# Changes between parts of the TensorE array, weighed by kind and put off by up to 100 places, in a macaron transformer kernel

## The chip, the core and the metric

The kernel runs on one core of one Trainium2 chip. A core has engines that run their own instruction streams and wait for one another by semaphores: TensorE (PE in the profile; its weight loads are the row PEld) multiplies matrices into PSUM, a buffer of eight banks; VectorE (DVE), ScalarE (ACT) and GpSimd (POOL) work on vectors; SyncE (SP) issues DMAs. The metric is the time of one execution on the device in microseconds (us), as the median of several runs. All data is 32-bit floating point.

## The reference

The input `x` is eight sequences of 512 tokens with 256 channels. Three residual parts follow one another, each on a layer-normalized copy:

```python
x = x + 0.5 * _L0_ffn_ref(_layernorm(x), ...)
x = x + _L0_attn_ref(_layernorm(x), L0_attn_weight)
x = x + 0.5 * _L0_ffn_ref(_layernorm(x), ...)
```

`_L0_ffn_ref` is two layers of a local-attention block. In each, half of the channels are shifted by a token, a product with `wqkv` gives queries, keys and values for 8 heads of 64 channels, queries and keys are normalized, scaled and rotated, and each window of 128 tokens attends to itself and to the window before it. A product with `wo` is added; then comes a gated feed-forward part with 682 hidden channels (`w1`, GELU, `w2`).

`_L0_attn_ref` is global attention with 16 heads of 16 channels, in which queries and keys are the same: `scores = y @ y.T / 4`, a softmax over 512 tokens, a product with all 256 channels of the layer-normalized `x`, and for each head a 256x256 slice of `weight`, summed over the heads.

## The kernel before

**Streams.** The program is recorded first and ordered afterwards. Three generators record it: two block streams (`stream`, one for the even and one for the odd sequences), each with `attention` and `glu` for two layers, and the stream of the global heads (`global_heads`). They are stepped in turn, so that the records of all three are interleaved. The first block stream is six steps ahead of the second.

**Products and the parts of the array that they use.** TensorE is an array of 128x128. Most products use it whole: the product with `wqkv` (`front` in `attention`), with `wo` (`project`), with `w1` and `w2` (`glu`), the heads' products with `weight` (`project` in `global_heads`) and their weighted sums (`attend`), and the transposes. Three kinds use a part, and several of them run side by side in the array:

- scores of the local attention (`scores` in `attention`): 64 rows, two heads at a time; one recorded operation has four products and fills two PSUM banks. The last 42 hidden channels with their bias row (`glu`, 43 rows) belong to the same kind. This text calls it halves.
- probabilities times values (`values`): 64 columns, two heads at a time. Called columns.
- scores of the global heads (`scores` in `global_heads`): 16 rows, four products at a time into four banks. Called fours.

One product of the source is two instructions in the profile, and a transpose is one. What is recorded under `plan.together()` is one operation and is issued without a break.

**What follows the small products.** After local scores, VectorE adds the mask and takes row maxima, ScalarE computes the exponentials, and GpSimd (or VectorE) scales them. Except for the first and the last sequences of each stream, the probabilities are turned by VectorE and by DMAs through DRAM (`turned_far`); there, TensorE transposes them. The values product follows, then the product with `wo`. The probabilities have two buffers a stream, so the scores of the next tokens need those of the tokens before to have been used. After global scores, ScalarE computes four exponentials, which `attend` of that head reads; the exponentials have eight buffers, two heads' worth.

**The planner.** `Plan.order` is a list scheduler with a cost model (`Plan.cost`). Each operation has a rank, its place in the order of recording. The planner keeps a clock for each engine, and at each step it takes the engine whose earliest candidate can start first, then among the candidates that can start within 40 ns of that one it takes the lowest rank. To the rank, `STICK` places are added where the candidate needs a change of mode: on ScalarE another activation table, on TensorE another part of the array. `MODE` is the time that the planner's clock adds for such a change. The mode of a product is set in `cost`: before, it is "rows" for up to 64 rows, "columns" for up to 64 columns and "whole" otherwise, so that halves and fours are one mode. A candidate that opens more than four buffers and whose inputs are ready, which the scores of a global head are, holds back all candidates of a higher rank that open a PSUM bank (`hold`).

The order that comes out is fixed for all five queues, SyncE's DMA issues among them, and each engine runs its own in that order.

Of the kernel before, what the change touches and what calls it, by code (L numbers as in the profile page):

```python
# [167 lines left out]
def elements(a):  # L168
    n = 1
    for d in a.shape[1:]:  # L170
        n *= d
    return n


class Plan:
    ENGINES = ("tensor", "vector", "scalar", "gpsimd", "sync")
    SIGNAL = 110.0
    TABLE = 1283.0
    STICK = {"tensor": 4, "scalar": 12, "vector": 0, "gpsimd": 0, "sync": 0}
    MODE = 130.0  # L180

    def __init__(self):
        self.ops, self.stream, self.group, self.shift = [], None, None, 0.0
# [46 lines left out]
    def cost(self, op):  # L230

        if op.engine == "tensor":

            lanes, op.mode = {}, "whole"
            for name, args, kw in op.calls:
                lane, t = 0, 109.0
                if name == "matmul":
                    a = kw["lhsT"]
                    lane, t = (a.region()[0], args[0].region()[0]), 2 * max(0.842 * elements(kw["rhs"]), 109.0)
                    op.mode = "rows" if a.shape[0] <= 64 else "columns" if a.shape[1] <= 64 else "whole"  # L240
                lanes[lane] = lanes.get(lane, 0.0) + t
            busy = max(lanes.values())
            return busy, busy + 170
        name, args, kw = op.calls[0]
        n = max(elements(a) for a in (*args, *kw.values()) if hasattr(a, "shape"))
        if name == "dma_start":
            return 580.0, 2300.0
        if op.engine == "scalar":
            if name == "activation":
                op.mode = {AF.Exp: "exp", AF.Gelu: "gelu"}.get(args[2])  # L250
                busy = 70 + 0.82 * n + (105 if "bias" in kw else 0)
                return (busy + 93, busy + 310) if "accum_out" in kw else (busy, busy + 110)
            return 70 + 0.81 * n, 175 + 0.81 * n
        if op.engine == "vector":
            if name == "tensor_tensor_reduce":
                return 90.0 + n, 250.0 + n
            if name == "bn_stats":
                return 70.0 + n, 150.0 + n
            return 90 + 1.035 * n, 170 + 1.035 * n
        if name == "memset":  # L260
            return 80 + 0.85 * n, 100 + 0.85 * n
        if ALU.pow in args:
            return 350.0 + 157 * n, 400.0 + 157 * n
        return 210 + 1.98 * n, 250 + 1.98 * n

    def order(self):

        for op in self.ops:
            op.busy, op.done = self.cost(op)
            op.waits = len(op.after)  # L270
            for o in op.after:
                o.before.append(op)

            for t in op.tiles:
                if t.users[0] is op:
                    source = [] if t.ring.space == PSUM else [u for u in op.tiles if u.ring.space == PSUM and u.users[0] is not op]
                    (source[0].users[0] if source else op).opens.append(t)
        for op in self.ops:
            op.opens.sort(key=lambda t: t.turn)
            for t in op.opens:  # L280
                for o in t.users:
                    if o is not op:
                        op.admits.append(o)
                        o.waits += 1
        free, mode = dict.fromkeys(self.ENGINES, 0.0), dict.fromkeys(self.ENGINES)
        pipe = 0.0
        candidates = {e: [op for op in self.ops if op.engine == e and not op.waits] for e in self.ENGINES}
        order = []

        def slots(op):  # L290

            need, turns, at = {}, {}, 0.0
            for t in op.opens:
                k, i = need.get(t.ring, 0), turns.get((t.ring, t.stream), 0)
                need[t.ring], turns[t.ring, t.stream] = k + 1, i + 1
                if t.ring.space != PSUM:

                    k += t.ring.missing(t.stream, t.turn) - i
                if len(t.ring.free) <= k:
                    return None  # L300
                at = max(at, t.ring.free[k][0])
            return at

        while len(order) < len(self.ops):
            best = None
            for e in self.ENGINES:
                when = []
                hold = min((op.rank for op in candidates[e] if len(op.opens) > 4 and op.ready <= free[e]), default=None)
                for op in candidates[e]:
                    if op.opens:  # L310
                        at = slots(op)
                        if at is None:
                            continue
                        if hold is not None and op.rank > hold and op.opens[0].ring.space == PSUM:
                            continue
                        at = max(at, op.ready, free[e])
                    else:
                        at = max(op.ready, free[e])
                    when.append((at, op))
                if when:  # L320
                    t = min(at for at, _ in when)
                    if best is None or t < best[0]:
                        best = t, e, when
            assert best is not None, "the plan is stuck"
            t, e, when = best
            change = {"tensor": self.MODE, "scalar": self.TABLE}.get(e, 0.0)
            switch = lambda op: change if op.mode is not None and op.mode != mode[e] else 0.0
            at, op = min(
                ((at, op) for at, op in when if at <= t + 40), key=lambda c: (c[1].rank + (self.STICK[e] if switch(c[1]) else 0), c[0])
            )  # L330
            candidates[e].remove(op)
            op.start = at + switch(op)
            mode[e] = op.mode or mode[e]
            free[e] = op.start + op.busy
            op.end = op.start + op.done
            if op.calls[0][0] == "dma_start":
                a = op.calls[0][2]["out"]
                pipe = max(pipe, op.start + 2000.0) + elements(a) * a.shape[0] * 4 / 170
                op.end = pipe + 300
            for x in op.opens:  # L340
                _, x.slot = x.ring.free.pop(0)
                x.ring.open(x.stream, x.turn)
            for x in op.tiles:
                x.left -= 1
                x.end = max(x.end, op.end)
                if not x.left:
                    x.ring.free.append((x.end + self.SIGNAL, x.slot))
                    x.ring.free.sort()
            for o in op.before:
                if o.engine != e:  # L350
                    o.ready = max(o.ready, op.end + self.SIGNAL)
                elif e != "tensor":
                    o.ready = max(o.ready, op.end)
            for o in op.before + op.admits:
                o.waits -= 1
                if not o.waits:
                    candidates[o.engine].append(o)
            order.append(op)
        return order
# [661 lines left out]
```

## Time and profile before

| | |
|---|---|
| median of 3 runs | 4,106.5 us (4,104.8 to 4,114.1) |
| profiled execution | 4,109.5 us |
| its span, first to last instruction | 4,107.8 us |
| granted TensorE clock, mean | 0.996 of full speed |
| TensorE instructions | 19,968 matmuls, 4,028.8 us busy |
| VectorE, ScalarE, GpSimd busy | 2,479.5, 1,866.7, 1,291.2 us |
| mean share of the DMA engines, main queue | 29.0% |

How to read it: an engine's busy time is the union of its instructions' records. For TensorE the ends of the records are modelled, so how close its instructions follow one another is read from their starts. In the groups and in the order of time, `128*64 128x128` says that 128 rows and 64 columns of the array are used, and that the result is 128 partitions by 128 elements; `psum_bank<-work_p,work_v` names the output and the inputs by the tiles of the program. Since all instructions are issued from one helper, all have the line L365, and the tiles tell them apart: `work_kT,work_qT` are local scores, `work_p,work_v` and `work_pT,work_v` are values, `work_hT` are global scores, `work_xw,work_e` is `attend`, `work_wa,work_gz` is the heads' product with `weight`, `wpool_w` is the feed-forward part and `wpool_wqkv` and `wpool_wo` are the products around local attention. What stands in brackets is idle time ahead of an instruction and what ended it.

### The profile page before, as it was taken

The page shows a single profiled execution, that of the slowest core. Times are in us where ns is not written, and L with a number is a line of the kernel's source. Part 1 is how long each engine was busy: PE and PEld are TensorE (multiplying, and loading weights), DVE is VectorE, ACT ScalarE, POOL GpSimd, SP SyncE. Part 2 cuts the span into 40 slices and gives each one's busy share as a digit, 9 for nine tenths or more (in the row PEclk, how much of TensorE's full clock was granted, in tenths as well). Part 3 has the DMA queues.
Part 4 walks back from the last instruction along what each step waited for, and adds up shares of the span by engine and source line. Part 5 has one row for each costly group of instructions (what it writes and reads, how often), then busy time and mean ns, then how long its engine had stood idle before and what let it go on. Part 6 is the DMA issues. An engine that isn't in the chain of part 4 may idle for free.

```text
span 4107.8 us, 59405 instructions
## 1 busy us (share of the span) xinstructions
PE 4028.8 (98%) x19968; PEld 2739.1 (67%) x19968; DVE 2479.5 (60%) x6760; ACT 1866.7 (45%) x4606; POOL 1291.2 (31%) x1147
## 2 busy tenths in 40 slices
PE   7999999999999999999999999999999999999998
PEld 4565676666666667666676766667676666686655
DVE  7575655756557565574756656567547565535574
ACT  5665444444444344443444544444324344323664
POOL 5242423424234232341523324234214232103140
PEclk9999999999999999999999999999999999999999
DMA  3001433423334243342433423334224243210000
GB/s 112 1 22 45 126 113 104 137 88 121 117 105 147 63 132 110 100 158 70 148 115 98 157 74 118 113 108 151 81 60 148 77 136 100 67 33 11 1 22 11
DMA packets 378704, 379.93 MB, mean 92 GB/s; under 512 B 48320, under 2 KB 323360, under 8 KB 378400
## 3 DMA queue, kind: packets, MB, share of 16 engines
q1 hardware_dynamic: 377536, 374.81, 29.0%
q8 instruction: 159, 2.61, 0.3%
q10 hardware_dynamic: 864, 1.33, 0.1%
q14 instruction: 145, 1.19, 0.1%
HBM read 216.61 MB, written 142.61 MB: 87 GB/s over the span
## 4 chain that ended last, share of the span: by engine, by line
PE 81%; DVE 9%; ACT 6%; issue 2%; POOL 1%; DMA 0%; SPq 0%; DVEq 0%; ACTq 0%; POOLq 0%
PE psum_bank L365 81%; ACT work_p L365 3%; DVE work_qn L365 3%; DVE work_p L365 2%; DVE small_ss L365 1%; ACT L365 1%; DVE work_both L365 0%; POOL small_rn L365 0%; DVE xpool_x L365 0%; ACT work_qn L365 0%; DVE small_nmax L365 0%; DVE small_bnst L365 0%; POOL work_t L365 0%; DVE zpool_z L365 0%; SPq L365 0%
## 5 line engine op out<-in xcount | busy, mean ns | idle before, releaser
L365 PE MATMUL psum_bank<-work_xw,work_e 128*128 128x256 f32 x4096 | 977.5, 384 | 6.8 <-DVE work_xw L365 4.3
L365 PEld LDWEIGHTS psum_bank<-work_xw,work_e 128*128 128x128 f32 x4096 | 759.4, 190 | 203.0 <-issue 67.4
L365 PE MATMUL psum_bank<-wpool_wqkv,zpool_z 128*128 128x512 f32 x1536 | 705.1, 599 | 3.3 <-DVE xpool_x L365 1.5
L365 ACT ACTIVATE work_p<-work_p,small_nmax,small_rn 128x256 f32<-128x256 f32 (+1 forms) x1024 | 574.2, 563 | 284.4 <-DVE small_nmax L365 146.9
L365 POOL TENSOR_TENSOR work_t<-work_qn,const_tab 128x256 f32<-128x256 f32 x512 | 391.1, 785 | 700.0 <-ACT work_qn L365 698.5
L365 POOL TENSOR_TENSOR work_p<-work_p,small_ri 128x1024 f32<-128x1024 f32 (+1 forms) x192 | 334.5, 1744 | 834.3 <-DVE small_ri L365 370.3
L365 PE MATMUL psum_bank<-zpool_z,wpool_w 128*128 128x512 f32 x1280 | 566.0, 596 | 1.4 <-DVE zpool_z L365 1.4
L365 ACT ACTIVATE work_e<-psum_bank 128x512 f32<-128x512 f32 x512 | 297.9, 595 | 485.3 <-PE psum_bank L365 480.8
L365 POOL TENSOR_TENSOR small_rn<-small_ss,const_nhalf 128x8 f32<-128x8 f32 x256 | 483.4, 1890 | 89.2 <-DVE small_ss L365 80.7
L365 PE MATMUL psum_bank<-work_wa,work_gz 128*128 128x256 f32 x2048 | 491.3, 383 | 10.1 <-DVE work_gz L365 5.6
L365 PEld LDWEIGHTS psum_bank<-wpool_wqkv,zpool_z 128*128 128x128 f32 x1536 | 284.4, 191 | 299.9 <-issue 273.6
L365 DVE SCALAR_TENSOR_TENSOR xpool_x<-psum_bank,gsmall_rinv,xpool_x 128x256 f32<-128x256 f32 x512 | 242.0, 474 | 343.1 <-PE psum_bank L365 340.4
L365 PEld LDWEIGHTS psum_bank<-work_wa,work_gz 128*128 128x128 f32 x2048 | 381.8, 190 | 82.5 <-issue 17.7
L365 PEld LDWEIGHTS psum_bank<-zpool_z,wpool_w 128*128 128x128 f32 x1280 | 240.5, 190 | 292.6 <-issue 263.6
L365 DVE CUSTOM_DVE_ANT_0 work_p<-psum_bank,const_mask 128x256 f32<-128x256 f32 (+1 forms) x1024 | 339.2, 383 | 46.6 <-PE psum_bank L365 45.2
L365 ACT COPY work_qn<-psum_bank 128x512 f32<-128x512 f32 x256 | 146.7, 582 | 363.0 <-PE psum_bank L365 328.4
L365 DVE COPY work_xw<-psum_bank 128x512 f32<-128x512 f32 x256 | 174.3, 682 | 156.2 <-PE psum_bank L365 155.9
L365 ACT ACT_TABLE_LOAD x158 | 202.7, 1283 | 143.2 <-DVE small_nmax L365 60.1
L365 DVE TENSOR_REDUCE small_ss<-work_sq 128x8 f32<-128x512 f32 x256 | 173.0, 676 | 145.3 <-ACT work_sq L365 145.0
L365 POOL TENSOR_TENSOR small_rstd<-small_ve,const_nhalf 128x4 f32<-128x4 f32 x48 | 49.8, 1037 | 648.1 <-DVE small_ve L365 616.1
L365 PE MATMUL psum_bank<-wpool_wo,work_o 128*128 128x256 f32 x1024 | 247.3, 385 | 2.5 <-ACT work_o L365 2.4
L365 PE MATMUL psum_bank<-wpool_w,work_p 128*128 128x256 f32 x1024 | 247.7, 385 | 0.0
(81 smaller groups left out, 5009.2 us busy)
## 6 DMA issues: line engine op xcount, KB each, us to landing
dram_turned<-work_p SPq DMA_DIRECT2D x144, 512.0 KB
work_p<-dram_turned SPq DMA_DIRECT2D x576, 128.0 KB
dram_turned<-work_both SPq DMA_DIRECT2D x96, 512.0 KB
work_both<-dram_turned SPq DMA_DIRECT2D x384, 128.0 KB
work_wa<-in_weight_dram SPq DMA_DIRECT2D x128, 256.0 KB
wpool_w<-in_w_dram SPq DMA_DIRECT2D x48, 640.0 KB
work_hT<-work_gz SPq DMA_DIRECT2D x512, 32.0 KB
dram_turned<-work_p SPq DMA_DIRECT2D x48, 256.0 KB
```

Source lines behind the costliest of these rows:

```text
L365: getattr(getattr(nc, op.engine), name)(*map(real, args), **{k: real(a) for k, a in kw.items()})
```

## The change

Three things change in the planner, and nothing in what is recorded. `STICK` for TensorE goes from 4 to 100 places. The mode of a product has four kinds in place of three: up to 32 rows are "fours", up to 64 "halves". And the time of a change is taken by the kind that is left: 150 ns, or 290 ns when fours are left, in place of 130 ns for all. The program has the same instructions in another order.

```diff
-    STICK = {"tensor": 4, "scalar": 12, "vector": 0, "gpsimd": 0, "sync": 0}
-    MODE = 130.0
+
+    STICK = {"tensor": 100, "scalar": 12, "vector": 0, "gpsimd": 0, "sync": 0}
+    MODE = {"whole": 150.0, "columns": 150.0, "halves": 150.0, "fours": 290.0}
...
-                    op.mode = "rows" if a.shape[0] <= 64 else "columns" if a.shape[1] <= 64 else "whole"
+                    k, m = a.shape
+                    op.mode = "fours" if k <= 32 else "halves" if k <= 64 else "columns" if m <= 64 else "whole"
...
-            change = {"tensor": self.MODE, "scalar": self.TABLE}.get(e, 0.0)
+            change = self.MODE.get(mode[e], 0.0) if e == "tensor" else self.TABLE if e == "scalar" else 0.0
```

The line behind the last one, which is as it was, makes a change of any candidate whose mode is not the engine's present one, and adds the stick to its rank.

## The prediction

> **What bounds the kernel now.** I read the page first: the busy shares, the chain that ended last, the groups by form; then the TensorE instructions in order of time, then the list of TensorE's waits.
>
> ```profile
> span 4107.8 us, 59405 instructions
> PE 4028.8 (98%) x19968; PEld 2739.1 (67%) x19968; DVE 2479.5 (60%) x6760; ACT 1866.7 (45%) x4606; POOL 1291.2 (31%) x1147
> ...
> PE 81%; DVE 9%; ACT 6%; issue 2%; POOL 1%; DMA 0%; SPq 0%; DVEq 0%; ACTq 0%; POOLq 0%
> ```
>
> TensorE is busy for 98% of the span, no other engine for more than 60%, and 81% of the chain runs over it. But its ends are modelled, so 98% does not say what fills the time. Start times do. These are the TensorE instructions of one stretch in order (start, length, what, count, idle before):
>
> ```profile
> 1511.04 1.89 PE L365 MATMUL psum_bank<-work_xw,work_e 128*128 128x256 f32 x8
> 1512.77 1.89 PE L365 MATMUL psum_bank<-work_wa,work_gz 128*128 128x256 f32 x8
> 1514.49 1.89 PE L365 MATMUL psum_bank<-work_xw,work_e 128*128 128x256 f32 x8
> 1516.31 1.09 PE L365 MATMUL psum_bank<-work_p,work_v 128*64 128x128 f32 x16
> 1517.34 1.14 PE L365 MATMUL psum_bank<-work_hT 16*128 16x512 f32 x8
> 1519.92 1.99 PE L365 MATMUL psum_bank<-work_wa,work_gz 128*128 128x256 f32 x8 [1.44 <-DVE xpool_x L365]
> 1521.85 1.09 PE L365 MATMUL psum_bank<-work_p,work_v 128*64 128x128 f32 x16
> 1522.87 3.72 PE L365 MATMUL psum_bank<-work_xw,work_e 128*128 128x256 f32 x16
> 1526.52 0.66 PE L365 MATMUL psum_bank<-work_p,work_v 128*64 128x128 f32 x8
> ```
>
> Eight instructions of 128x256 on the whole array take 1.73 us from start to start when whole products stand on both sides (1511.04 to 1512.77), so 0.216 us each. The eight ahead of a product on half the columns (128\*64) take 1.82 (1514.49 to 1516.31): 0.09 more. The sixteen between two half-column products take 3.65 (1522.87 to 1526.52) where 16 x 0.216 is 3.45: 0.10 for the second start after coming back, and 0.09 for leaving. That is the price of a change between parts of the array.
>
> I took the starts of all 19,968 matmul records in order and put each distance against that form's own. The distances are 0.216 (256 columns, whole), 0.429 (512), 0.109 (a transpose); products that share the array start 0.007 apart, and a pair then takes 0.216 or 0.112 (64 rows) or 0.109 (half columns), and four of 16 rows 0.429. By kind, the extra of a visit is:
> - columns: 0.093 + 0.051 on entering, 0.100 + 0.104 on returning, 0.35 us
> - halves (64 or 43 rows): 0.093 + 0.104 and 0.096 + 0.104, 0.40 us
> - fours (16 rows): 0.093 + 0.104 and 0.109 + 0.104, 0.41 us
>
> There are 1,055 changes: 489 excursions from the whole array, in which 208 runs of halves, 231 of columns and 127 of fours stand. Their extras add up to **196 us**, 0.185 each. The rest of the span: the work at its own distances 3,783 (8,704 x 0.216 + 2,816 x 0.429 + 1,536 x 0.109 + the small products' 527), ahead of the first matmul and after the last start 19, and 110 left over, which is waiting, 77 of it in 90 single waits. The sum is 4,107.8. Of those waits only 33 us lie between 300 and 3,700 us; the rest is the beginning and the end. TensorE is thus bound by its own issue, and changes are 4.8% of the span.
>
> ```profile
> PE psum_bank L365 <- DVE work_qn L365: 19.3, 19, 3.1
> PE psum_bank L365 <- DVE ypool_y L365: 16.2, 3, 12.8
> PE psum_bank L365 <- DVE xpool_x L365: 7.6, 7, 1.5
> ```
>
> (us in total, times, longest.) No wait is large, and the longest is the first.
>
> **The change, part by part.** It adds and removes no instruction. It changes the order that the planner writes out, on all five queues, since one engine's pick decides when the next one's inputs are ready.
>
> *The stick of 100 places.* A place is one recorded operation. There are about 16,100: DVE 6,760 less 1,024 accumulator reads, ACT 4,606 less 1,536 reads and 158 table loads, POOL 1,143, some 2,260 DMA issues on SP, and 4,060 on TensorE. So 100 places are 0.62% of the span, **25.5 us**; the 4 places of before are 1 us. Before, TensorE left the whole array for nearly any older small product, and 168 excursions are a single run of columns, 154 of halves, 94 of fours. Now it stays whole until a ready small product is 100 places older than every ready whole one, or until no whole one is ready. Meanwhile small products pile up and go together, and as all of them are changes by then, the next kind follows the first: k kinds cost k + 1 changes, not 2k.
>
> How many remain? The floor of one change is as it was; only the count moves. I cut the span into windows and let each be one excursion through the kinds that occur in it: windows of 25.5 us leave 497 changes, of 16 us 635, of 13 us 704. The full 25.5 us is reached by no average product: many are old when they become ready (a far block's probabilities come back by DMA), whole products run out at times, and the hold of the planner lets the heads' scores (fours, 128, one every 32 us) pass later-ranked bank users. I take the 16 us windows, **640 changes**: 415 fewer, 415 x 0.185 = **-77 us**. Ends: 497 (-103) and 900 (-29).
>
> *What the moved products drag along.* Scores and values come up to 25 us later, and so do their evictions (DVE row maxima, ACT exponentials, POOL scaling), the DMAs that SP issues for the turned probabilities (one of 512 KB and four of 128 KB for most pairs) and the next scores, which need the probabilities' buffers back. SP's queue is in order, so a late turn also stands ahead of later weight and head loads. All of this is hidden as long as TensorE has other whole products ready: its waits of 33 us in 3,400 show that it nearly always has. If that cover goes, a late value is next waited for by the projection and then by the feed-forward part of that block, at 1 to 3 us each, the longest of the first row above.
>
> *Bunching.* Here a rule of the Trainium skill speaks against the change. TensorEngine Tiling (Array Packing), under PSUM Bottleneck and Gotcha 1: PSUM Pressure, says that splitting the array speeds up TensorE but not the emptying of PSUM, and that row tiles fill different banks. The rows agree on sizes: a scores product fills two banks in 0.9 us and DVE empties them in 4 x 0.417 plus reads, 2.0 us; a head's scores fill four in 1.1 us and ACT needs 4 x (0.595 + 0.206) = 3.2 us:
>
> ```profile
> L365 ACT ACTIVATE work_e<-psum_bank 128x512 f32<-128x512 f32 x512 | 297.9, 595 | 485.3 <-PE psum_bank L365 480.8 <-issue 4.5
> ...
> L365 DVE CUSTOM_DVE_ANT_0 work_p<-psum_bank,const_mask 128x256 f32<-128x256 f32 x768 | 280.5, 417 | 34.8 <-PE psum_bank L365 33.5 <-DMA work_both<-dram_turned 0.3
> ```
>
> Two scores products and a head in a row take all eight banks. By the rule each of the 128 heads would then end in a wait like that at 1519.92 (1.44 us, columns and fours ahead of it): +184 us, and the whole would be 4,107.8 - 77 + 184 = 4,215. By the trace, the 50 excursions of two or three runs between 300 and 3,700 us already show what bunches do: they and the 3 us behind them hold 0.106 us of waits each, single ones 0.025. With some 200 excursions of mostly two or three runs, that is about 20 us in place of the 14 that lie there now; bunches get larger than today's, so I take **+20 us**, with 0 and +120 as ends. The measured rate weighs more than the rule, as DVE and ACT empty banks side by side and neither is over 60% busy.
>
> *The kinds and their prices* (rows split into halves and fours; 150 and 290 ns in place of 130). A change between halves and fours occurs 11 times now and costs 0.2 like any other, so treating it as one is right; the prices only move planned start times. They come nearer to the 0.185 measured. I cost this at 0, from -5 to +5.
>
> *ACT's rule* stays, so 158 table loads stay near that; at 1.28 us each they lie in ACT's idle 55%.
>
> Sum against the profiled execution: 4,107.8 - 77 + 20 = 4,050.8 of span, plus 1.7 around it (4,109.5 in all before). That execution is 3.0 above the median of the runs, 4,106.5; a difference of -57 makes **4,050**.
>
> **The rivals.**
> 1. *Fuller bunches without waits*: 497 changes and no new wait, -103: 4,003. For it: the backlog that the small number of waits shows. Against: the windows assume perfect batches.
> 2. *Bunches starve PSUM* (slower): -77 is 0.39 us for each of 200 excursions. If a wait of 1.5 us follows more than one in four, the gain is gone; at one in two, +150: 4,180. For it the rule and the line at 1519.92, against it 0.106 us as measured.
> 3. *Late streams*: the two block streams fall 25 us behind the heads, and the end, where only they are left and waits are dense already (12 us of the last 108 without a busy TensorE), grows by that; with the beginning +40, so 4,107 - 77 + 20 + 40, about 4,090. Against: when no whole product is ready, the rule does not hold a small one back.
> 4. *The order hardly changes*, because same-kind products are seldom ready: 950 changes, -19, so 4,087; with new waits of that size, no change. Against: whole products are ready nearly always, so most departures could have been put off.
>
> **How the numbers follow.** Forecast 0.54 (its own range 4,015 to 4,085), fuller bunches 0.15, starving 0.16, late streams 0.08, hardly a change 0.07. The range of 8 in 10 goes from 3,990, a little under rival 1 for windows wider than 25.5 us, to 4,135, where waits of 1.5 us follow a third of the excursions (+100). A measurement of this kernel tells about 0.2%, 8 us. Faster: 0.54 + 0.15 + 0.07 of late streams + 0.03 of rival 4, 0.79, less 0.04 for the forecast's own upper tail, 0.75. Same 0.06, the rest of rival 4 and a little. Slower 0.19: starving, and that tail.
>
> **What the changed profile would show.** Right: changes down to 550 to 750, each still at 0.18 to 0.21; runs of 32 and more columns instructions and of 24 and more halves in the order of time; instruction counts as before; TensorE's waits below 140 us in all. The starving rival: many lines with over 1 us of idle behind fours or halves, released by ACT work_e, DVE work_p or xpool_x. Late streams: the last 100 us longer with waits on work_qn and work_pT. What would make me wrong is a planner that meets the bunches with banks full, or a count that stays above 900.

## The result and the profile after

The changed kernel takes **4,056.0 us** (median of 4 runs, 4,055.9 to 4,056.2) against 4,105.9 us for the kernel before (here over 4 runs): a ratio of 0.9874 with a 95% interval of 0.9857 to 0.9891. The forecast was 4,050. The time is right; two terms of the sum behind it are not, and they cancel.

The head of the page of the changed kernel:

```profile
span 4054.2 us, 59391 instructions
PE 3986.8 (98%) x19968; PEld 2747.4 (68%) x19968; DVE 2461.8 (61%) x6760; ACT 1822.8 (45%) x4566; POOL 1277.5 (32%) x1147
```

The matmuls are the same 19,968. TensorE is still busy for 98% of the span, and its issue is still the bound: by the starts, work and changes fill 3,946 of the 4,054 us (table below). Its instructions in order of time, in about the same stretch as before (start, length, what, count; what was L365 is L367 now):

```profile
1513.32 1.14 PE L367 MATMUL psum_bank<-work_kT,work_qT 64*128 64x256 f32 x8
1514.38 1.09 PE L367 MATMUL psum_bank<-work_p,work_v 128*64 128x128 f32 x16
1515.41 1.99 PE L367 MATMUL psum_bank<-work_xw,work_e 128*128 128x256 f32 x8
1517.24 1.89 PE L367 MATMUL psum_bank<-work_wa,work_gz 128*128 128x256 f32 x8
1519.06 1.09 PE L367 MATMUL psum_bank<-work_p,work_v 128*64 128x128 f32 x16
1520.08 1.14 PE L367 MATMUL psum_bank<-work_hT 16*128 16x512 f32 x8
1521.15 1.99 PE L367 MATMUL psum_bank<-wpool_wo,work_o 128*128 128x256 f32 x8
```

Two things are seen. The price of a change is what it was: the eight products behind the columns take 1.83 us (1515.41 to 1517.24), 0.10 more than 1.73, and the eight ahead of the next columns 1.82. And small products of different kinds now stand behind one another (halves and columns, then columns and fours), so two kinds cost three changes. But the two products of columns, 4.7 us apart, were not brought together.

The list of TensorE's waits (us in total, times, longest):

```profile
PE psum_bank L367 <- DVE work_qn L367: 17.9, 35, 3.1
PE psum_bank L367 <- DVE ypool_y L367: 17.6, 6, 12.9
PE psum_bank L367 <- DVE work_p L367: 6.9, 3, 3.1
```

The first two rows are about as before, and the 7.6 us behind xpool_x are gone from the list.

I took the span apart as in the prediction, from the starts of all matmuls: 3,783 us of work at its own distances, changes, the ends, and what is left, which is waits and stretches at half clock. Where a wait covers a change, the change is counted here at its usual price (so 198 us for before, where the prediction had 196).

| kernel | changes | us in changes | ends | left over | of it, clock not granted | span |
|---|---|---|---|---|---|---|
| before | 1,055 | 197.9 | 18.6 | 108.4 | 16.5 | 4,107.8 |
| after | 885 | 162.9 | 19.6 | 88.8 | 11.4 | 4,054.2 |
| difference | -170 | -35.0 | +1.0 | -19.6 | -5.1 | -53.6 |

The clock column is one minus the mean granted clock, times the span; a little of it falls into waits or into the ends, so it is not wholly a part of what is left over. So 35 us of the gain came from fewer changes and 20 from less waiting and half clock. With one fixed price for each kind of change, taken from the prediction's list, the same traces give 34 and 21; in x4 below, the split would move by 7 us, in x8 by 6, in the others by less.

### The profile page after: what moved, and what is told of

It is laid out like the page before. It is cut to its first block, busy times and chain, and to the rows that moved or that the text cites. A ratio compares the mean times of both kernels' runs of the same rounds, so it can differ in the third digit from the quotient of the medians.

```text
span 4054.2 us, 59391 instructions
## 1 busy us (share of the span) xinstructions
PE 3986.8 (98%) x19968; PEld 2747.4 (68%) x19968; DVE 2461.8 (61%) x6760; ACT 1822.8 (45%) x4566; POOL 1277.5 (32%) x1147
## 4 chain that ended last, share of the span: by engine, by line
PE 45%; DVE 3%; ACT 2%; POOL 1%; issue 0%; DMA 0%; SPq 0%; DVEq 0%; ACTq 0%; POOLq 0%
PE psum_bank L367 45%; ACT work_p L367 1%; DVE work_p L367 1%; DVE work_qn L367 1%; POOL small_rn L367 0%; DVE ypool_y L367 0%; DVE small_ss L367 0%; DVE xpool_x L367 0%; POOL work_t L367 0%; DMA work_both<-dram_turned 0%; DVE small_bnst L367 0%; POOL small_rstd L367 0%; ACT work_pT L367 0%; ACT work_qn L367 0%; ACT work_sq L367 0%
## 5 line engine op out<-in xcount | busy, mean ns | idle before, releaser
L367 PE MATMUL psum_bank<-work_xw,work_e 128*128 128x256 f32 x4096 | 957.1, 383 | 3.9 <-DVE work_xw L367 1.9
L367 PEld LDWEIGHTS psum_bank<-work_xw,work_e 128*128 128x128 f32 x4096 | 761.0, 190 | 190.5 <-issue 52.1
L367 ACT ACTIVATE work_p<-work_p,small_nmax,small_rn 128x256 f32<-128x256 f32 (+1 forms) x1024 | 574.0, 562 | 295.3 <-DVE small_nmax L367 218.4
L367 PE MATMUL psum_bank<-wpool_wqkv,zpool_z 128*128 128x512 f32 x1536 | 703.9, 596 | 0.3 <-ACT zpool_z L367 0.3
L367 POOL TENSOR_TENSOR work_p<-work_p,small_ri 128x1024 f32<-128x1024 f32 (+1 forms) x192 | 327.3, 1707 | 1038.2 <-DVE small_ri L367 595.6
L367 POOL TENSOR_TENSOR work_t<-work_qn,const_tab 128x256 f32<-128x256 f32 x512 | 383.9, 770 | 755.4 <-ACT work_qn L367 748.9
L367 PE MATMUL psum_bank<-zpool_z,wpool_w 128*128 128x512 f32 x1280 | 559.6, 595 | 1.5 <-DVE zpool_z L367 1.4
L367 POOL TENSOR_TENSOR small_rn<-small_ss,const_nhalf 128x8 f32<-128x8 f32 x256 | 484.2, 1893 | 129.9 <-DVE small_ss L367 124.1
L367 PE MATMUL psum_bank<-work_wa,work_gz 128*128 128x256 f32 x2048 | 475.5, 380 | 2.1 <-DVE work_gz L367 1.3
L367 DVE SCALAR_TENSOR_TENSOR xpool_x<-psum_bank,gsmall_rinv,xpool_x 128x256 f32<-128x256 f32 x512 | 242.1, 475 | 386.3 <-PE psum_bank L367 383.6
L367 ACT ACTIVATE work_e<-psum_bank 128x512 f32<-128x512 f32 x512 | 298.5, 596 | 395.7 <-PE psum_bank L367 386.1
L367 PEld LDWEIGHTS psum_bank<-wpool_wqkv,zpool_z 128*128 128x128 f32 x1536 | 284.2, 191 | 274.8 <-issue 256.2
L367 PEld LDWEIGHTS psum_bank<-zpool_z,wpool_w 128*128 128x128 f32 x1280 | 242.5, 191 | 301.8 <-issue 274.9
L367 PEld LDWEIGHTS psum_bank<-work_wa,work_gz 128*128 128x128 f32 x2048 | 384.4, 190 | 67.9 <-issue 10.2
L367 DVE CUSTOM_DVE_ANT_0 work_p<-psum_bank,const_mask 128x256 f32<-128x256 f32 (+1 forms) x1024 | 339.2, 385 | 115.5 <-PE psum_bank L367 114.6
L367 ACT COPY work_qn<-psum_bank 128x512 f32<-128x512 f32 x256 | 148.6, 583 | 426.3 <-PE psum_bank L367 368.5
L367 DVE TENSOR_REDUCE small_ss<-work_sq 128x8 f32<-128x512 f32 x256 | 173.3, 677 | 176.5 <-ACT work_sq L367 176.2
L367 DVE SCALAR_TENSOR_TENSOR work_p<-psum_bank,const_vec,work_p 128x512 f32<-128x512 f32 x128 | 95.9, 750 | 263.4 <-PE psum_bank L367 162.4
L367 PE MATMUL psum_bank<-wpool_wo,work_o 128*128 128x256 f32 x1024 | 248.4, 386 | 0.9 <-ACT work_o L367 0.7
L367 DVE COPY work_xw<-psum_bank 128x512 f32<-128x512 f32 x256 | 173.9, 680 | 116.0 <-PE psum_bank L367 114.7
L367 PE MATMUL psum_bank<-wpool_w,work_p 128*128 128x256 f32 x1024 | 242.9, 380 | 0.4 <-ACT work_e L367 0.4
L367 PE MATMUL psum_bank<-work_kT,work_qT 64*128 64x256 f32 (+1 forms) x2048 | 236.1, 364 | 1.8 <-DVE work_xw L367 1.4
```

Of the source, the lines that this page charges most:

```text
L367: getattr(getattr(nc, op.engine), name)(*map(real, args), **{k: real(a) for k, a in kw.items()})
```

## The experiments

All are orders of the same work: they compute everything. "Changes" and "left over" are taken from each one's trace as above. Time is the median, and the ratio is to the kernel before on the same chip. Each trace is one execution, and the twenty executions of x12 alone lie between 4,110.3 and 4,117.1 us, so a few us of what is left over say nothing.

| run | stick | prices, ns | changes | us in changes | left over | clock not granted | us | ratio (95%) |
|---|---|---|---|---|---|---|---|---|
| x8 | -100 | 130 | 1,379 | 255.2 | 81.1 | 14.4 | 4,136.3 | 1.0069 (1.0053 to 1.0085) |
| x12 | 2 | 130 | 1,056 | 199.9 | 112.5 | 23.1 | 4,114.6 | 1.0016 (1.0009 to 1.0023) |
| x2 | 4 | by kind | 1,059 | 198.2 | 109.2 | 14.8 | 4,108.9 | 0.9998 (0.9989 to 1.0007) |
| x5 | 50 | 130 | 940 | 173.7 | 96.4 | 14.9 | 4,073.2 | 0.9911 (0.9894 to 0.9929) |
| x6 | 99 | 130 | 872 | 161.3 | 75.7 | 7.9 | 4,042.6 | 0.9838 (0.9823 to 0.9853) |
| x1 | 100 | 130 | 874 | 161.4 | 72.6 | 6.4 | 4,039.7 | 0.9828 (0.9809 to 0.9847) |
| x3 | 100 | 130, four kinds | 890 | 163.9 | 84.3 | 12.9 | 4,050.9 | 0.9855 (0.9836 to 0.9875) |
| x11 | 100 | as measured | 876 | 161.0 | 107.6 | 16.8 | 4,073.4 | 0.9914 (0.9899 to 0.9929) |
| x7 | 150 | 130 | 817 | 151.6 | 98.5 | 18.3 | 4,056.2 | 0.9871 (0.9855 to 0.9886) |
| x10 | 150 | as measured | 804 | 148.5 | 93.2 | 11.4 | 4,047.3 | 0.9853 (0.9836 to 0.9869) |
| x9 | 175 | as measured | 817 | 149.4 | 97.1 | 8.3 | 4,051.7 | 0.9862 (0.9848 to 0.9877) |
| x4 | no limit | by kind | 751 | 135.1 | 155.4 | 35.5 | 4,091.4 | 0.9957 (0.9941 to 0.9973) |

### The parts of the change alone

Theory A: the stick does all, through the number of changes. Theory B: the prices by kind bring the planned clock nearer to the chip's, and so the waits fell. The stick alone, x1:

```diff
-    STICK = {"tensor": 4, "scalar": 12, ...}
+    STICK = {"tensor": 100, "scalar": 12, ...}
     MODE = 130.0
```

> The kernel before with the stick of 100 places alone (rows stay one kind, 130 ns for every change). Its order has 874 changes, 11 fewer than the changed kernel's 885. Theory A, the stick does it all by the number of changes, and the drop of 20 us in waits comes with it or by chance: about 4,054 us, changes 160 us, waits near 90. Theory B, the prices by kind bring the planned clock nearer to the chip's and so take the waits down: changes 160 us as well, but waits stay near 110, about 4,073 us.

4,039.7 us, better than either theory said and better than the whole change. The head of its page and its list of waits:

```profile
span 4036.4 us, 59364 instructions
```

```profile
PE psum_bank L365 <- DVE ypool_y L365: 18.7, 7, 12.8
PE psum_bank L365 <- DVE work_qn L365: 13.6, 21, 3.1
PE psum_bank L365 <- ACT work_pT L365: 7.3, 11, 1.6
```

The changes cost what they do in the changed kernel (161 and 163 us); what is left over is 16 us less. The first line has one wait of 12.8 us at the beginning that all kernels have (12.8 in before, 12.9 after, 13.6 in x4), so what shrinks lies elsewhere.

Kinds and prices alone, x2:

```diff
-    STICK = {"tensor": 100, "scalar": 12, ...}
+    STICK = {"tensor": 4, "scalar": 12, ...}
```

> The changed kernel with the stick back at 4 places: four kinds and the prices of 150 and 290 ns alone. Its order has 1,059 changes, as many as before (1,055). Theory A: about 4,106 us, as before. Theory B: changes 196 us, waits near 90, about 4,087 us.

The same as before within 0.1%: as many changes, and as much left over. Theory B falls: with a stick of 4, the prices by kind took no wait away.

The changed kernel with one price, x3:

```diff
-    MODE = {"whole": 150.0, "columns": 150.0, "halves": 150.0, "fours": 290.0}
+    MODE = {"whole": 130.0, "columns": 130.0, "halves": 130.0, "fours": 130.0}
```

> The changed kernel with 130 ns for every change, the four kinds and the stick of 100 kept; 890 changes in its order. Theory A: 4,057 us. Theory B: waits back near 110, about 4,075 us.

4,050.9 us; waits do not go back up. Against B again. With x1 and x2 this puts the gain on the stick.

### No limit

x4 puts small products off until nothing else can start:

```diff
-    STICK = {"tensor": 100, "scalar": 12, ...}
+    STICK = {"tensor": 100000, "scalar": 12, ...}
```

> The changed kernel with a stick without limit: TensorE leaves a part of the array only when nothing of that kind can start. 751 changes in its order, 134 fewer. If the number of changes sets the time and waits stay at 90: 134 x 0.183 = 25 us less, about 4,031 us. If bunches and late streams cost waits once small products are put off without limit: waits of 130 us and more, 4,070 us or above.

4,091.4 us: 28 us saved in changes against the changed kernel, and 67 more left over. This run settles two points. First, by its rule TensorE leaves a part of the array only when nothing of that kind can start, and 751 changes are still made. So it is not the number of places that keeps bunches small. The planner of this kernel, followed step by step, says what does. At 233 of its 462 departures from a part, no other product of that kind is a candidate (not all that it needs has been placed in the order yet); at 63 there is one that can start only more than 40 ns later; at 166 there is one without a free buffer, and 117 of these are heads' scores, which lack mostly one of the eight buffers of the exponentials. Second, this run shows the rival of starved PSUM at work. The waits of this run, and its order of time around 1,285 us, where a new sequence of the heads' stream begins:

```profile
PE psum_bank L367 <- ACT work_e L367: 11.3, 6, 2.8
```

```profile
1283.12 1.99 PE L367 MATMUL psum_bank<-wpool_wo,work_o 128*128 128x256 f32 x8
1285.05 3.80 PE L367 MATMUL psum_bank<-work_hT 16*128 16x512 f32 x14
1291.63 2.07 PE L367 MATMUL psum_bank<-work_hT 16*128 16x512 f32 x2 [2.78 <-ACT work_e L367]
1293.63 0.47 PE L367 MATMUL psum_bank<-const_ident,ypool_y 128*128 128x128 f32 x1
```

Two heads' scores in a row fill eight banks, and the last product waits until ScalarE has emptied one. The kernel before has such a place too, at 1,311 us, with a shorter wait:

```profile
1311.05 2.05 PE L365 MATMUL psum_bank<-work_hT 16*128 16x512 f32 x10
1314.05 2.27 PE L365 MATMUL psum_bank<-work_hT 16*128 16x512 f32 x6 [0.95 <-ACT work_e L365]
```

The stages of x4, from 1,281 us on (busy us and count of each engine, then the granted clock, DMA share and GB/s), show what follows:

```profile
1281.00:1285.00 4.00, 3.88 (x24) 2.90 (x24) 2.83 (x8) 2.57 (x5) 3.89 (x5) 1.00 0.49 164
1285.00:1289.00 4.00, 3.85 (x15) 1.48 (x14) 4.00 (x19) 2.77 (x9) 1.17 (x2) 0.94 0.79 258
1289.00:1293.00 4.00, 1.37 (x2) 0.50 (x2) 4.00 (x6) 4.00 (x15) 2.52 (x2) 0.50 0.48 131
1293.00:1297.00 4.00, 4.00 (x10) 2.75 (x10) 2.75 (x5) 3.62 (x12) 3.46 (x2) 0.50 0.74 243
```

The clock is granted at half, and stays so for 10.2 us. Near 804, 2,125 and 3,442 us the order of time has nearly the same picture, with one transpose between the two heads, and each time a wait of 2.23 us. In all this run loses 35 us of clock, 24 more than the changed kernel. The waits on work_e (11 us) and the half clock behind these four places (17 us) are at most 28 of the 67 us; the rest is spread over other waits, and its cause is not shown.

### How far, and how much is chance

Theory C: the stick itself takes waits down as far as it puts small products off. Theory D: waits differ from order to order by chance. x5, x6, x7 and x8 are the kernel before with other sticks:

```diff
-    STICK = {"tensor": 4, "scalar": 12, ...}
+    STICK = {"tensor": 50, "scalar": 12, ...}
```

> The kernel before with a stick of 50; 940 changes in its order, 115 fewer than before, so 21 us less in changes. Theory C, the stick itself takes waits down as far as it puts small products off: about half of the 36 us that a stick of 100 took from the waits, so about 4,067 us. Theory D, waits differ from order to order by chance: anything between 4,050 (rest as with 100) and 4,085 (rest as before).

4,073.2 us, 12 of 36 us of waits gone. Theory C had 18 of them gone and is 6 us off; theory D allowed nearly anything, so this run does not decide between them.

```diff
+    STICK = {"tensor": 99, "scalar": 12, ...}
```

> The kernel before with a stick of 99 in place of 100: nearly the same rule, another order, 872 changes (874 with 100). Theory C: within 4 us of 4,040. Theory D, waits are a matter of chance: the rest outside work and changes may lie anywhere from 73 to 90 us, so 4,040 to 4,057; then the 16 us between the stick alone and the whole change say nothing of kinds and prices.

4,042.6 us, 3 us of left-over from x1: as theory C said, but inside the range of theory D as well.

```diff
+    STICK = {"tensor": 150, "scalar": 12, ...}
```

> The kernel before with a stick of 150; 817 changes, 57 fewer than with 100, so 11 us less in changes. If waits stay at 73: about 4,029 us. If they turn up beyond 100 places, as they did without a limit (155): half-way would be 4,060 us or more.

4,056.2 us: the 57 changes fewer than x1 save 10 us, as priced, and waits and clock give back 26. Waits turn up again, by about a third of the way to x4.

```diff
+    STICK = {"tensor": -100, "scalar": 12, ...}
```

> The kernel before with a stick of minus 100 places, so that TensorE prefers a change: 1,379 changes, 324 more than before. At 0.186 us each that is 60 us more. If changes alone set the time: 4,167 us. If each small product that goes early also keeps the streams ahead, waits fall and it is less, down to 4,130; if the order is bad for waits too, 4,190.

4,136.3 us. The 324 additional changes cost 57 us, which the price gave as 60. But what is left over fell by 27 us too, with a stick of the other sign, as the second case of the expectation had it (small products that go early keep the streams ahead); that reason was not tested. The fall speaks against theory C as a rule.

x12 takes a stick of 2 in place of 4:

```diff
+    STICK = {"tensor": 2, "scalar": 12, ...}
```

> The kernel before with a stick of 2 in place of 4: 1,056 changes, as before, in another order. If the waits of before belong to a small stick: rest of 105 to 112, 4,105 to 4,112 us. If they were that one order's: rest anywhere from 73 to 109, down to 4,070 us.

4,114.6 us, left over 112.5. With x2 that makes three orders with a small stick and 108 us or more: the waits of before were not the bad luck of its one order.

### The prices as measured

x9, x10 and x11 price a change in the planner as the trace shows it:

```diff
+    LEAVE = {"whole": 93.0, "columns": 100.0, "halves": 96.0, "fours": 109.0}
+    ENTER = {"whole": 104.0, "columns": 51.0, "halves": 104.0, "fours": 104.0}
...
+                return self.LEAVE.get(mode[e], 0.0) + self.ENTER[op.mode]
```

> The changed kernel with each change priced as the trace shows it: the part left (whole 93, columns 100, halves 96, fours 109 ns) plus the part entered (51 for columns, 104 for the others), and a stick of 175. 817 changes, so 152 us. Theory E, a planned clock that is right about changes meets fewer waits: rest of 70 us or less, about 4,025 us. Theory D, waits are a matter of the single order: rest between 73 and 109, so 4,028 to 4,064.

> The same prices with a stick of 150: 804 changes, 149 us. Theory E: about 4,022 us. Theory D: 4,026 to 4,062; the stick of 150 with the old prices had a rest of 98.

> The same prices with the stick of 100 of the change: 876 changes, 162 us. Theory E: rest of 70 or less, 4,035 us or less, below the stick alone with 130 ns (4,040). Theory D: 4,038 to 4,074.

4,051.7, 4,047.3 and 4,073.4 us. Theory E falls, and all three lie where theory D put them: with the stick of 100 the measured prices leave 107.6 us over, where the flat 130 ns left 84.3 with the same four kinds (x3) and 72.6 with three (x1). A planned clock that was nearer to the trace about changes did not meet fewer waits.

**What is settled and what is open.** In all 14 orders a change costs 0.180 to 0.189 us, from 751 changes to 1,379. What is left over is 108 to 113 us in the three orders with a stick of 2 or 4, 73 to 108 in the eight with 99 to 175, 96 with 50, 81 with -100 and 155 without a limit. So a stick near 100 tends to bring fewer waits, but among orders with 872 to 890 changes it still runs from 73 to 108. Why one of them meets fewer waits than another is not settled; with that spread, the 16 us between x1 and the whole change cannot be put down to kinds or to prices. The best kernel is x1, the stick alone, with x6 level within the intervals: 0.9828 (0.9809 to 0.9847), ahead of the whole change's 0.9874 (0.9857 to 0.9891).

## Why the prediction was right, and where it was not

**The bound and the price of a change: right.** TensorE's issue is the bound in all runs (work and changes fill 96 to 98% of each span), and a change cost 0.184 us in the changed kernel (0.185 in the sum).

**How many changes remain: wrong.** The step cut the span into windows and let each be one excursion through the kinds in it; 16 us gave 640 changes. There are 885, and -77 us became -35. The step took it that waiting products of a kind go together. They hardly did: runs of small products went from 566 to 525 only (columns 231 to 235, halves 208 to 164, fours 127 to 126). What fell is the number of excursions, 489 to 360, because kinds now follow one another: excursions of two or more runs went from 73 to 134. The same 16 us windows on the changed kernel's trace give 603, so it was the rule of one excursion for each window that failed, not its length; x4 shows that even no limit leaves 751. The planner of the changed kernel shows why bunches stay small: at 284 of its 524 departures from a part no other product of that kind is a candidate, at 86 one can start only more than 40 ns later, and at 151 one has no free buffer. Only 3 are made because an older product outweighs the stick.

**Bunching: wrong in sign, and the trace was nearer than the rule.** +20 us was taken; waits and half clock fell by 20. The excursions of two or more runs between 300 and 3,700 us hold about 0.02 us of waits each (0.106 before), with the 3 us behind them. That is some 2 us in all where there were 5, so only about 3 of the 20 us lie at the bunches; where the rest comes from is open. The prediction took 184 us from the Trainium skill's TensorEngine Tiling (Array Packing), PSUM Bottleneck, which says only that emptying PSUM is not sped up and may become the bottleneck; one wait for each head was the prediction's own reading, and it did not come. In x4, where bunches had no limit, that mechanism is there, at the start of a sequence, with waits of 2 to 3 us.

**So the two errors, 42 us too much and 40 us too little, cancel.** The forecast of 4,050 owes its nearness to that, which is luck.

**Kinds and prices at 0: right alone** (x2, 0.9998), but with the stick they belong to an order 16 us slower than x1, beyond the 5 us allowed.

**ScalarE's table loads: wrong, without effect.** They were to stay near 158. The group of the changed kernel has 118:

```profile
L367 ACT ACT_TABLE_LOAD x118 | 151.4, 1283 | 33.9 <-DMA wpool_wqkv<-in_wqkv_dram 14.8 <-issue 9.8 <-PE psum_bank L367 5.0
```

That is 51 us less of ScalarE's time. ScalarE is busy for 45% of the span and not the bound; x4 has fewer still, 94, and is slower.

**The rivals.** Fuller bunches (497 changes): no. Starved PSUM: not here, but in x4. Late streams: no; single waits (of over 0.25 us) after 3,700 us are 22.6 us in both kernels, and the ends grew by 1 us. Hardly a change (950): its count was the nearest to 885, and its reason, that products of one kind are seldom ready together, is the larger part of what the planner shows; it forecast 4,087 because it had 65 changes more (12 us) and no fall in waits (20 us).

**What the profile was to show.** Changes at 0.18 to 0.21 us each: yes, 0.184. Waits below 140 us: yes, 89. Runs of 24 and more instructions of halves: from 1 to 20, yes. Runs of 32 and more of columns: from 17 to 10, no. 550 to 750 changes: no.

## What to carry to other kernels

Where one engine issues without pause, take the distances between the starts of its instructions and put each against its form's own: the price of a change came out to a few nanoseconds, and it held over 14 orders. The number of changes that a rule of order leaves is much harder to forecast: ask not how long a product may wait, but whether a second one of its kind comes ready in that time and finds a free buffer. And when a planner's rule is tuned, try each of its parts alone and some neighbours of each number, since orders with the same number of changes differed here by 34 us (4,039.7 to 4,073.4), about twice what lies between the stick alone and the whole change.

## What the runs showed of the hardware that was not expected

TensorE's clock goes to half in stretches of 3.41 us or a multiple of it (3.41, 6.83 or 10.24 us in all 14 traces, but for the one that the end of each trace cuts off), and a stretch can begin without a wait of that length. In the kernel before one begins at 2,542 us behind a single wait of 1.46 us. In x1 one begins at 1,286 us with only 0.18 us of idle time in the 3.4 us ahead of it, where two heads' 16-row scores had just run:

```profile
1281.63 1.98 PE L365 MATMUL psum_bank<-work_hT 16*128 16x512 f32 x10
1283.79 2.28 PE L365 MATMUL psum_bank<-work_hT 16*128 16x512 f32 x6 [0.18 <-DMA work_p<-dram_turned]
1286.00 6.27 PE L365 MATMUL psum_bank<-work_xw,work_e 128*128 128x256 f32 x20
```

Whether products of few rows count for less in what lets the clock fall is not shown by this one place. The sum of what was not granted goes from 6 us (x1) to 35 us (x4). So a wait that lets the clock fall can cost more than its own length: in x4 the single waits are some 30 us longer in all than in the changed kernel, and the clock takes 24 us more, part of it while TensorE waits anyway. The prediction's price of a wait left that out.
